# Expert stage of a two-attention, two-expert network: 1/sum on VectorE, variances as columns, single norm pieces, first combination tiles begun in the second sweep

## Chip, core and metric

The kernel runs on one core of one Trainium2 chip. The metric is the device time of one execution in microseconds (us), as the median of several runs. Lower is better.

## What is computed

The reference takes x of 4096 tokens by 256 features, in float32, and adds four branches to it, one after another, each on the layer norm of what came before:

```
x = x + attention_a(layernorm(x))
x = x + experts(layernorm(x))
x = x + attention_b(layernorm(x))
x = x + experts(layernorm(x))
```

Both attentions are causal with 16 heads. The expert branch is the same both times, with the same weights. It has 64 experts with 32 slots each, so 2048 columns in all:

```
logits = (x @ phi_w.T + phi_b).reshape(8, 512, 64, 32)
D = softmax(logits, over the 32 slots)        # dispatch
C = softmax(logits, over the 64 experts)      # combination
X_tilde = clip(einsum('tznp,tzd->npd', D, x), -33000, 65000)
X_tilde = tanh(normalised X_tilde over d: (X - mu) * rsqrt(var + 1e-5))
Y_tilde = einsum('npd,ndH->npH', X_tilde, expert_w) + expert_b
out     = einsum('tznp,npH->tzH', C, Y_tilde)
```

## The kernel before

The 4096 tokens are 32 tiles (NT) of 128 rows (P); x stays on chip. Four stages follow one another: attention a, experts, attention b, experts. Both expert stages run the same class, `_Experts` (lines 607 to 975). The first ends in statistics and queries for attention b; the second writes `out`.

**Order.** TensorE's instructions are kept in the program's order (helpers `mm`, line 66, and `tr`, line 69). All others (VectorE, ScalarE, GpSimd and the DMA issues on SyncE, called SP) are ordered by the framework's scheduler when the kernel is built. It may move an issue ahead of or behind its neighbours. Each engine then runs its own list strictly in order. Pieces of work can be put into a queue, `side`, and `beside` (line 79) takes one piece from it per call.

**Norm and sweeps.** The layer norm of x is cut into pieces of four tiles: statistics (line 91 on), the roots, the scaling on ScalarE, and two transposes of two tiles each. A transpose goes into a bank (line 72), the only one in its PSUM pool, and is copied to `xnT` on ScalarE (line 753). Two groups of four tiles are normed ahead; 36 pieces go into `side`. Then there are two sweeps over the 32 tiles, one for each half h of the 2048 columns. In each step:

- `logits(h, t)` makes 128 x 1024 logits, with the bias added by VectorE (line 775), stores them to DRAM (`ld`), takes the maximum of each expert's slots, subtracts it on GpSimd (line 783), and takes the exp on ScalarE. VectorE also takes the column maxima `cm`.
- `divide(h, t)` sums (line 796), takes the reciprocal and multiplies on GpSimd (line 798).
- Four products accumulate X_tilde in PSUM (`acc`).

Logits run two tiles ahead of the accumulation, divide one. After the first sweep the norm of half 0 of X_tilde and its expert products are pieces beside the second sweep.

**Norm of X_tilde.** `centre` gets the mean over features by a matmul with a matrix of 1/256, subtracts on VectorE and squares on GpSimd. `spread` gets the variance likewise, in all 128 rows at once, and takes the root and, on 128 x 512 elements, the reciprocal (line 702). `squash` multiplies on GpSimd (line 707) and takes tanh. `product(ec)` multiplies 128 slots by the weights of four experts; its result goes through the one bank to `ys` (line 720).

**Combination.** It runs over the 32 tiles:

- `combine_begin(t)` loads the tile's logits `l` back (1 MB, line 805), then the 128 KB of x as it was ahead of the branch, `xl` (line 809), takes the maximum of both halves (`mc`, line 811), subtracts it on GpSimd in two halves (line 815) and takes the exp (line 818).
- `combine_sums(t)` sums over experts on VectorE (`sc`, line 824), takes the reciprocal (line 825), and copies it fourfold on GpSimd (line 827).
- `turn(t)` transposes the reciprocals (`rT`), copies them on ScalarE (line 835), and transposes e in 16 pieces (`ps`). VectorE multiplies both to `lT` (line 842).
- `weigh(t)` multiplies `lT` by `ys` in 16 products; VectorE adds `xl` and writes x (line 860). The second stage then issues the store of `out` (line 862); the first takes statistics.

Begin and sums run two tiles ahead of weigh, turn one. The buffers are two of `l`, three of e, two of `lT`, four of `ps`; `xl` and the small tiles come from a pool with four buffers of each. Tiles 0 and 1 are begun at the second-last step of the second sweep. The first turn and half of the first weigh lie between the steps of half 1's norm.

Of the kernel before, what the change touches and what calls it, by code (L numbers as in the profile page):

```python
# [606 lines left out]
class _Experts:  # L607
# [8 lines left out]
    def __init__(self, net, phiT, phi_b, ew, eb, out=None, attention=None):  # L616
        self.net, self.phiT, self.phi_b = net, phiT, phi_b
        self.ew, self.eb, self.out = ew, eb, out
        self.attention = attention
        self.phi = net.zone[:, 0 : 2 * E].rearrange("p (c e) -> p c e", c=2)  # L620
        self.phb = net.zone[:, 2 * E : 3 * E]

    def load(self):
        nc, EH = self.net.nc, E // 2
        for h in range(2):
            for c in range(2):
                nc.sync.dma_start(
                    self.phi[:, c, ts(h, EH)], self.phiT[ts(c, P), ts(h, EH)]
                )
            nc.sync.dma_start(  # L630
                self.phb[:, ts(h, EH)],
                self.phi_b[ts(h, EH)].rearrange("(o e) -> o e", o=1).partition_broadcast(P),
            )

    def run(self):
# [10 lines left out]
        with ExitStack() as ctx:  # L646
# [4 lines left out]
            sp = pool("ff_s", 4)  # L651
            net.banks = pool("psm", 1, space=PSUM)
# [3 lines left out]
            nc.gpsimd.memset(mean, 1.0 / D)  # L656
            ys = [cp.tile([P, NC2, D], F32, name="ys0"), None]
# [8 lines left out]

            def load_w(ec, w=None):
                if w is None:
                    w = ewp.tile([P, 4, 2, D], F32, name="w")
                nc.sync.dma_start(w, ew[ts(ec, 4)].rearrange("n (c p) h -> p n c h", p=P))  # L670
                ews[ec] = w

            def load_b(h):
                b = rp.tile([P, NC2, D], F32, name="ebt")
                for j in range(4):
                    nc.sync.dma_start(
                        b[ds(32 * j, 32), :, :],
                        eb.rearrange("(o c j) h -> j o c h", o=1, j=4)[j][:, ts(h, NC2), :]
                        .partition_broadcast(32),
                    )  # L680
                ebs[h] = b

            sqs = {}

            def centre(n):
                xs = xt[:, :, ts(n, 512)]
                mu = net.bank()
                for d in range(2):
                    mm(mu, mean, xs[:, d, :], start=d == 0, stop=d == 1)
                sq = ewk.tile([P, 2, 512], F32, name="sq")  # L690
                for d in range(2):
                    nc.vector.tensor_tensor(xs[:, d, :], xs[:, d, :], mu, ALU.subtract)
                    nc.gpsimd.tensor_tensor(sq[:, d, :], xs[:, d, :], xs[:, d, :], ALU.mult)
                sqs[n] = sq

            def spread(n):
                sq = sqs[n]
                var = net.bank()
                for d in range(2):
                    mm(var, mean, sq[:, d, :], start=d == 0, stop=d == 1)  # L700
                nc.scalar.activation(sq[:, 0, :], var, AF.Sqrt, bias=net.eps)
                nc.vector.reciprocal(sq[:, 0, :], sq[:, 0, :])

            def squash(n):
                xs = xt[:, :, ts(n, 512)]
                for d in range(2):
                    nc.gpsimd.tensor_tensor(xs[:, d, :], xs[:, d, :], sqs[n][:, 0, :], ALU.mult)
                nc.scalar.activation(xs, xs, AF.Tanh)

            def product(ec):  # L710
                w = ews.pop(ec)
                y = net.bank()[:, 0:D]
# [20 lines left out]
            def norm_pieces(j):  # L733
                def stats(i2):
                    for t in (4 * j + 2 * i2, 4 * j + 2 * i2 + 1):
                        net.stats(t)
                    if i2:
                        net.roots(4 * j, 4 * j + 4)

                def scale():  # L740
                    for t in range(4 * j, 4 * j + 4):
                        nc.scalar.activation(
                            x[:, t, :], x[:, t, :], AF.Identity,
                            bias=shift[:, t : t + 1], scale=rstd[:, t : t + 1],
                        )

                def turn(i2):
                    t2 = 2 * j + i2
                    pt = net.bank().rearrange("p (c i t) -> p c i t", c=2, i=2)
                    for i in range(2):  # L750
                        for c in range(2):
                            tr(pt[:, c, i, :], x[:, 2 * t2 + i, ts(c, P)])
                    nc.scalar.copy(
                        xnT[:, :, ts(t2, 2 * P)], pt.rearrange("p c i t -> p c (i t)")
                    )

                return [
                    lambda: stats(0), lambda: stats(1), scale, lambda: None,
                    lambda: turn(0), lambda: turn(1),
                ]  # L760
# [4 lines left out]
            def logits(h, t):  # L765
                l = lp.tile([P, NH, SLOT], F32, name="l")
                lf = l.rearrange("p n s -> p (n s)")
                for n in range(2):
                    lg = pl.tile([P, 512], F32, name="lg")
                    for c in range(2):  # L770
                        mm(
                            lg, xnT[:, c, ts(t, P)], phi[:, c, ds(h * EH + n * 512, 512)],
                            start=c == 0, stop=c == 1,
                        )
# [3 lines left out]
                nc.sync.dma_start(ld[t][:, h, :], lf)  # L778
# [22 lines left out]
            ce, css, lTs, xls, pools = {}, {}, {}, {}, {}  # L801

            def combine_begin(t):
                l = pools["l"].tile([P, NEXP, SLOT], F32, name="l")
                nc.sync.dma_start(
                    l.rearrange("p n s -> p (n s)"), ld[t].rearrange("p h e -> p (h e)")
                )
                xl = sp.tile([P, D], F32, name="xl")
                nc.sync.dma_start(xl, xd[:, t, :])
                m = sp.tile([P, SLOT], F32, name="mc")  # L810
                nc.vector.tensor_tensor(m, cm[:, t, 0, :], cm[:, t, 1, :], ALU.max)
                e = pools["e"].tile([P, NEXP, SLOT], F32, name="e")
                for h in range(2):
                    ns = ts(h, NH)
                    nc.gpsimd.tensor_tensor(  # L815
                        e[:, ns, :], l[:, ns, :], _bc(m.unsqueeze(1), [P, NH, SLOT]), ALU.subtract
                    )
                    nc.scalar.activation(e[:, ns, :], e[:, ns, :], AF.Exp)  # L818
                ce[t], xls[t] = e, xl


            def combine_sums(t):
# [4 lines left out]
                nc.gpsimd.tensor_copy(s4, _bc(s.unsqueeze(1), [P, 4, SLOT]))  # L827
# [39 lines left out]
            for j in range(2):  # L867
                for f in norm_pieces(j):
                    f()
            for j in range(2, NT // 4):  # L870
                net.side.extend(norm_pieces(j))
# [4 lines left out]
            for n, (h, t) in enumerate(seq):  # L876
# [7 lines left out]
                if n + 1 < len(seq):  # L884
                    divide(*seq[n + 1])
                if n == len(seq) - 2:

                    nctx.close()
                    pools["e"] = pool("fc_w", 2)
                    pools["l"] = pool("fc_l", 1)  # L890
                    pools["lT"] = pool("fc_t", 1)
# [7 lines left out]
                if n < len(seq) - 2:  # L899
                    for _ in range(2 if h == 0 else 1):  # L900
                        net.beside(3)
# [15 lines left out]
                if n == len(seq) - 2:  # L917
                    assert not net.side and not net.urgent and not net.agenda
                    load_b(1)
                    for k in range(3):  # L920
                        load_w(
                            NC2 + 3 + k,
                            net.zone[:, ts(k, E)].rearrange("p (n c h) -> p n c h", n=4, c=2),
                        )
                    for k in range(2):
                        combine_begin(k)
                        combine_sums(k)
# [4 lines left out]
            load_w(NEC - 2, pool("ff_wx", 1, rctx, side="right").tile([P, 4, 2, D], F32, name="wx"))  # L932
            pools["r"] = pool("fc_r", 1, space=PSUM)
            pools["t"] = pool("fc_p", 4, space=PSUM)
            pools["o"] = pool("fc_o", 2, space=PSUM)
            centre(2)
            centre(3)
            turn(0)
            spread(2)
            spread(3)  # L940
            weigh(0, 0, NC2)
            squash(2)
            squash(3)
            for ec in range(NC2, NEC):
                product(ec)
                if ec == NC2:
                    load_w(NEC - 1)
# [4 lines left out]
            for t in range(NT):  # L952
                if t + 2 < NT:
                    combine_begin(t + 2)
                if t == 0:
                    weigh(0, NC2, NEC)
                if t + 1 < NT:
                    turn(t + 1)
                if t + 2 < NT:
                    combine_sums(t + 2)  # L960
                if t > 0:
                    weigh(t, 0, NEC)
# [104 lines left out]
```

## Time and profile before

| | |
|---|---|
| median of 3 runs | 5329.53 us (5329.0 to 5331.33) |
| the profiled execution's own time | 5322.71 us |
| its span | 5321.0 us |
| granted TensorE clock | 0.983 |
| first expert stage, in the span | about 1780 to 2674 us |
| second expert stage | about 4436 to 5321 us |
| TensorE, VectorE, ScalarE, GpSimd busy | 94, 78, 49, 23% |

The tables and lines of the profile come from one execution. A row of a group has the line of the program, the engine, the operation, what it writes and reads with shapes, the count, then total busy us and the mean in ns, and the idle time of the engine ahead of it with what ended that. PE is TensorE, PEld its weight loads, DVE is VectorE, ACT ScalarE, POOL GpSimd and SPq the DMA issues of SyncE. A row of a window has the stretch in us, its length, the busy us of each engine with its instructions in brackets, the granted clock of TensorE as a share of full speed, the share of time in which the DMA engines worked, and GB/s. A row of the timeline has the start in us, the duration, the engine, and what was done; in square brackets stands how long the engine had been idle and for whom. A row of waits has the sum in us, the count and the longest.

### The profile page before, as it was taken

The page shows a single profiled execution, that of the slowest core. Times are in us where ns is not written, and L with a number is a line of the kernel's source. Part 1 is how long each engine was busy: PE and PEld are TensorE (multiplying, and loading weights), DVE is VectorE, ACT ScalarE, POOL GpSimd, SP SyncE. Part 2 cuts the span into 40 slices and gives each one's busy share as a digit, 9 for nine tenths or more (in the row PEclk, how much of TensorE's full clock was granted, in tenths as well). Part 3 has the DMA queues.
Part 4 walks back from the last instruction along what each step waited for, and adds up shares of the span by engine and source line. Part 5 has one row for each costly group of instructions (what it writes and reads, how often), then busy time and mean ns, then how long its engine had stood idle before and what let it go on. Part 6 is the DMA issues. An engine that isn't in the chain of part 4 may idle for free.

```text
span 5321.0 us, 79263 instructions
## 1 busy us (share of the span) xinstructions
PE 5025.3 (94%) x29824; PEld 2663.5 (50%) x29824; DVE 4142.4 (78%) x7742; ACT 2608.9 (49%) x3036; POOL 1208.7 (23%) x1178
## 2 busy tenths in 40 slices
PE   7999999999999899979989999999999998999799
PEld 4444454545454344447744454444454543444577
DVE  5788998989987478767757888989899864787665
ACT  3566666666677412122235666666666674111221
POOL 3211000000000345454411110000000003455443
PEclk9999999999999999989989999999999999999899
DMA  6433221222211211443353342222222112113432
GB/s 248 140 111 121 74 68 63 69 63 63 62 59 42 85 68 67 138 142 113 119 199 130 105 128 68 66 70 61 63 63 67 56 36 86 67 75 135 143 129 90
DMA packets 265584, 499.16 MB, mean 94 GB/s; under 512 B 44880, under 2 KB 109904, under 8 KB 257008
## 3 DMA queue, kind: packets, MB, share of 16 engines
q1 hardware_dynamic: 259968, 485.57, 27.5%
q10 hardware_dynamic: 4896, 7.87, 0.4%
q8 instruction: 234, 3.83, 0.3%
q14 instruction: 150, 1.23, 0.1%
q0 software_dynamic: 336, 0.66, 0.0%
HBM read 336.73 MB, written 156.76 MB: 93 GB/s over the span
## 4 chain that ended last, share of the span: by engine, by line
PE 65%; DVE 14%; POOL 11%; ACT 4%; issue 4%; DMA 1%; SPq 0%; DVEq 0%; POOLq 0%; ACTq 0%
PE bank L67 20%; PE o L67 20%; PE sc L67 17%; POOL e L815 5%; DVE mx L386 4%; DVE sc L824 4%; PE lg L67 3%; POOL e L783 3%; PE acc L67 3%; DVE junk L380 2%; POOL e L798 2%; ACT e L786 2%; DVE l L775 1%; ACT e L818 1%; ACT pb L462 1%
## 5 line engine op out<-in xcount | busy, mean ns | idle before, releaser
L462 ACT ACTIVATE pb<-sc 128x1024 f32<-128x1024 f32 (+3 forms) x2304 | 2071.0, 951 | 1093.2 <-PE sc L67 1090.3
L386 DVE TENSOR_REDUCE mx<-bank 128x1 f32<-128x512 f32 x3584 | 2223.2, 681 | 169.9 <-PE bank L67 165.7
L67 PE MATMUL bank<-k,q 64*128 64x512 f32 (+3 forms) x4608 | 1350.0, 452 | 72.8 <-DVE mx L386 29.9
L67 PEld LDWEIGHTS bank<-k,q 64*128 64x128 f32 x4608 | 666.5, 185 | 1178.6 <-DVE mx L386 780.3
L67 PE MATMUL o<-pb,va 128*32 128x512 f32 (+3 forms) x9216 | 1158.2, 574 | 0.9 <-POOL pb L466 0.7
L67 PE MATMUL sc<-q,k 64*128 64x512 f32 (+3 forms) x4608 | 988.1, 390 | 9.9 <-ACT pb L462 9.4
L67 PE MATMUL sc<-qm,one 64*128 64x512 f32 (+3 forms) x4608 | 946.9, 376 | 0.0
L466 POOL TENSOR_SCALAR_AFFINE_SELECT pb<-pb 128x256 f32<-128x256 f32 x512 | 205.7, 408 | 2260.5 <-ACT pb L462 2254.8
L380 DVE CUSTOM_DVE_ANT_0 junk<-bank,maskw 128x128 bf16<-128x128 f32 (+3 forms) x1024 | 501.6, 490 | 259.1 <-PE bank L67 151.8
L67 PEld LDWEIGHTS sc<-q,k 64*128 64x128 f32 x4608 | 508.8, 186 | 138.4 <-ACT pb L462 99.8
L67 PEld LDWEIGHTS sc<-qm,one 64*128 64x128 f32 x4608 | 525.6, 186 | 66.6
L786 ACT ACTIVATE e<-e 128x1024 f32<-128x1024 f32 x128 | 135.2, 1056 | 786.3 <-POOL e L783 786.3
L67 PE MATMUL acc<-e,x 128*128 128x512 f32 x1024 | 472.1, 605 | 35.2 <-POOL e L798 33.6
L67 PE MATMUL lg<-zone,xnT 128*128 128x512 f32 x1024 | 469.3, 602 | 0.2
L67 PE MATMUL o<-ys,lT 128*128 128x256 f32 x2048 | 453.0, 379 | 0.0
L67 PEld LDWEIGHTS o<-ys,lT 128*128 128x128 f32 x2048 | 384.5, 190 | 51.8 <-issue 2.0
L818 ACT ACTIVATE e<-e 128x1024 f32<-128x1024 f32 x128 | 135.3, 1057 | 459.3 <-POOL e L815 449.6
L67 PEld LDWEIGHTS acc<-e,x 128*128 128x128 f32 x1024 | 197.9, 194 | 290.5 <-issue 242.4
L798 POOL TENSOR_TENSOR e<-e,s 128x1024 f32<-128x1024 f32 x128 | 244.7, 1913 | 385.7 <-DVE s L797 385.7
L67 PEld LDWEIGHTS o<-pb,va 128*32 128x32 f32 x9216 | 182.9, 108 | 285.8 <-issue 263.2
L67 PEld LDWEIGHTS lg<-zone,xnT 128*128 128x128 f32 x1024 | 194.9, 193 | 242.5 <-issue 229.5
L815 POOL TENSOR_TENSOR e<-l,mc 128x1024 f32<-128x1024 f32 x128 | 299.6, 2363 | 24.1 <-DVE x L860 17.1
(101 smaller groups left out, 3234.9 us busy)
## 6 DMA issues: line engine op xcount, KB each, us to landing
k<-ak SPq DMA_DIRECT2D x144, 512.0 KB
k<-bk SPq DMA_DIRECT2D x144, 512.0 KB
ld<-l SPq DMA_DIRECT2D x128, 512.0 KB
l<-ld SPq DMA_DIRECT2D x64, 1024.0 KB
w<-in_L_ffn_expert_w_dram SPq DMA_DIRECT2D x24, 1024.0 KB
q<-aq SPq DMA_DIRECT2D x32, 512.0 KB
rb<-dd SPq DMA_DIRECT2D x64, 256.0 KB
q<-bq SPq DMA_DIRECT2D x32, 512.0 KB
```

Of the source, the lines that this page charges most:

```text
L67: self.tc.keep_in_program_order(self.nc.tensor.matmul(*a, **k))
L380: nc.vector.tensor_tensor_reduce(out=junk[:, 0:w], in0=scs[h2][:, 0:w], in1=maskw[:, QB - w : QB], scale=1.0, scalar=-3e38, op0=ALU.add, o ...
L386: nc.vector.tensor_reduce(m, scs[h2], AX.X, ALU.max)
L462: nc.scalar.activation(pb[:, :, off:QB], sc[:, :, off:QB], AF.Exp)
L466: nc.gpsimd.affine_select(out=d, in_=d, compare_op=ALU.is_ge, fill=0.0, base=0, pattern=[[0, 2], [1, P]], channel_multiplier=-1,)
L775: nc.vector.tensor_tensor(lf[:, ts(n, 512)], lg, phb[:, ds(h * EH + n * 512, 512)], ALU.add)
L783: nc.gpsimd.tensor_tensor(e, l, _bc(m.unsqueeze(2), [P, NH, SLOT]), ALU.subtract)
L786: nc.scalar.activation(ef, ef, AF.Exp)
L798: nc.gpsimd.tensor_tensor(e, e, _bc(s.unsqueeze(2), [P, NH, SLOT]), ALU.mult)
L815: nc.gpsimd.tensor_tensor(e[:, ns, :], l[:, ns, :], _bc(m.unsqueeze(1), [P, NH, SLOT]), ALU.subtract)
L818: nc.scalar.activation(e[:, ns, :], e[:, ns, :], AF.Exp)
L824: nc.vector.tensor_reduce(s, ce[t].rearrange("p n s -> p s n"), AX.X, ALU.add)
```

## The change

It affects `_Experts` alone. In words:

- The fourfold copy of 1/sum goes from GpSimd to VectorE.
- Layer norm: one piece norms four tiles, one piece transposes two; 20 pieces are queued. The first two transposes use the PSUM buffers of the logits. `beside` is called ahead of the accumulation in each step, and once more behind it in the first sweep.
- Norm of X_tilde: squares on ScalarE; variances as columns of 128 x 1 by tiny matmuls, with root and reciprocal on 128 x 4; they are put on a diagonal on VectorE and spread over the rows by a matmul with ones; VectorE multiplies from PSUM.
- The products of half 1 alternate between two PSUM banks.
- Tile 0 of the combination is begun in step 24 of the second sweep, in memory that half 0 of `phi` has left; tile 1 at the second-last step; tile 2 between the norm of half 1 and its products. In the main loop the beginning and the sums run three tiles ahead instead of two.
- `xl` has a pool of its own with four buffers; `ps` has three buffers instead of four.
- The DMAs of the expert stage, apart from `out` and from the loads of phi, go through a new helper that keeps them in the program's order on SP.

The diff, cut to its core:

```diff
-        self.phi = net.zone[:, 0 : 2 * E].rearrange("p (c e) -> p c e", c=2)
+        self.phi = net.zone[:, 0 : 2 * E].rearrange("p (h c e) -> p h c e", h=2, c=2)
...
+            xlp = pool("ff_xl", 4)
...
+            one = cp.tile([P, P], F32, name="one")
+            nc.gpsimd.memset(one, 1.0)
...
+            def dma(o, i):
+                tc.keep_in_program_order(nc.sync.dma_start(o, i))
...
-                    nc.gpsimd.tensor_tensor(sq[:, d, :], xs[:, d, :], xs[:, d, :], ALU.mult)
+                nc.scalar.activation(sqs[n], xs, AF.Square)
...
-                for d in range(2):
-                    mm(var, mean, sq[:, d, :], start=d == 0, stop=d == 1)
-                nc.scalar.activation(sq[:, 0, :], var, AF.Sqrt, bias=net.eps)
-                nc.vector.reciprocal(sq[:, 0, :], sq[:, 0, :])
+                for k in range(4):
+                    for d in range(2):
+                        mm(
+                            var[:, k : k + 1], sq[:, d, ts(k, P)], mean[:, 0:1],
+                            start=d == 0, stop=d == 1,
+                        )
+                r = sp.tile([P, 4], F32, name="rx")
+                nc.scalar.activation(r, var[:, 0:4], AF.Sqrt, bias=net.eps)
+                nc.vector.reciprocal(r, r)
+                nc.vector.tensor_tensor(
+                    sq[:, 0, :].rearrange("p (k e) -> p k e", k=4),
+                    _bc(net.ident.unsqueeze(1), [P, 4, P]), _bc(r.unsqueeze(2), [P, 4, P]),
+                    ALU.mult,
+                )
...
+                rs = net.bank()
+                mm(rs, one, sqs[n][:, 0, :], start=True, stop=True)
-                    nc.gpsimd.tensor_tensor(xs[:, d, :], xs[:, d, :], sqs[n][:, 0, :], ALU.mult)
+                    nc.vector.tensor_tensor(xs[:, d, :], xs[:, d, :], rs, ALU.mult)
...
-                nc.sync.dma_start(ld[t][:, h, :], lf)
+                dma(ld[t][:, h, :], lf)
...
+            def maxima(t):
+                cms[t] = sp.tile([P, SLOT], F32, name="mc")
+                nc.vector.tensor_tensor(cms[t], cm[:, t, 0, :], cm[:, t, 1, :], ALU.max)
+                xls[t] = xlp.tile([P, D], F32, name="xl")
+                dma(xls[t], xd[:, t, :])
...
+                dma(l.rearrange("p n s -> p (n s)"), ld[t].rearrange("p h e -> p (h e)"))
+                maxima(t)
...
-                nc.gpsimd.tensor_copy(s4, _bc(s.unsqueeze(1), [P, 4, SLOT]))
+                nc.vector.tensor_copy(s4, _bc(s.unsqueeze(1), [P, 4, SLOT]))
...
+            norm(0)
+            norm(1)
+            turn_x(0, first)
+            turn_x(1, first)
+            for j in range(2, NT // 2):
+                if j % 2 == 0 and j > 2:
+                    net.side.append(lambda j=j: norm(j // 2))
+                net.side.append(lambda j=j: turn_x(j))
...
+                if (h, t) == (1, 24):
...
+                    ce[0], l = z(0, E), z(2 * E, EH)
+                    maxima(0)
+                    for h2 in range(2):
+                        dma(l.rearrange("p n s -> p (n s)"), ld[0][:, h2, :])
+                        exponentials(0, ce[0], l, h2)
+                    combine_sums(0)
...
-            pools["t"] = pool("fc_p", 4, space=PSUM)
+            pools["t"] = pool("fc_p", 3, space=PSUM)
...
-                if t + 2 < NT:
-                    combine_begin(t + 2)
+                if t + 3 < NT:
+                    combine_begin(t + 3)
...
-                if t + 2 < NT:
-                    combine_sums(t + 2)
+                if t + 3 < NT:
+                    combine_sums(t + 3)
```

## The prediction

> **What bounds the kernel now.** I read the page first: the share of each engine, then the chain that ended last, to see whether TensorE is short of work or held up.
>
> ```profile
> PE 5025.3 (94%) x29824; PEld 2663.5 (50%) x29824; DVE 4142.4 (78%) x7742; ACT 2608.9 (49%) x3036; POOL 1208.7 (23%) x1178
> ...
> PE 65%; DVE 14%; POOL 11%; ACT 4%; issue 4%; DMA 1%; SPq 0%; DVEq 0%; POOLq 0%; ACTq 0%
> ...
> L815 POOL TENSOR_TENSOR e<-l,mc 128x1024 f32<-128x1024 f32 x128 | 299.6, 2363 | 24.1 <-DVE x L860 17.1
> ```
>
> TensorE is busy 94% of the span, yet the chain runs outside it for 35%, and GpSimd, busy 23% overall, carries 11% of the chain. The last row says where: the combination's exponent on GpSimd hardly ever waits. The change touches only the two expert stages (1780 to 2674 and 4436 to 5321 us), so I asked for windows of the first.
>
> ```profile
> core 0: us, PE busy (x) PEld busy (x) DVE busy (x) ACT busy (x) POOL busy (x), PEclk, DMA share, GB/s
> 1800.00:2050.00 250.00, 231.90 (x569) 106.11 (x570) 184.47 (x203) 44.63 (x51) 121.51 (x66) 0.98 0.23 87
> 2290.00:2350.00 60.00, 35.77 (x219) 20.77 (x218) 29.63 (x35) 10.82 (x12) 22.67 (x17) 0.86 0.39 135
> 2350.00:2460.00 110.00, 94.72 (x499) 81.03 (x499) 87.16 (x109) 35.33 (x45) 60.56 (x37) 0.95 0.39 131
> ```
>
> TensorE idles 18 us of the first sweep, 24 of the transition between the sweeps and the combination, and some 14% of the combination's start. The waits of TensorE name the causes: in the first sweep (first line) the norm's transposes wait for ScalarE's copy out of the one bank; in the combination (other two) for VectorE, and once, 11 us long, for GpSimd's copy.
>
> ```profile
> PE bank L70 <- ACT xnT L753: 14.0, 6, 2.7
> ...
> PE ps L70 <- DVE lT L842: 12.1, 18, 1.0
> PE rT L70 <- POOL s L827: 11.0, 1, 11.0
> ```
>
> Last came the timeline of one combination tile in the second expert stage.
>
> ```profile
> 5198.90 0.36 DVE L860 TENSOR_TENSOR x<-o,xl 128x256 f32<-128x256 f32 x1
> 5199.11 0.29 POOL L827 COPY s<-sc 128x128 f32<-128x128 f32 x1 [5.34 <-DVE sc L825]
> ...
> 5199.29 0.34 SPq L862 DMA_DIRECT2D out_dram<-x  x1
> 5199.36 4.69 POOL L815 TENSOR_TENSOR e<-l,mc 128x1024 f32<-128x1024 f32 x2
> 5199.68 0.43 SPq L809 DMA_DIRECT2D xl<-xd  x1
> ...
> 5204.08 0.32 SPq L805 DMA_DIRECT2D l<-ld  x1
> ...
> 5204.09 1.06 ACT L818 ACTIVATE e<-e 128x1024 f32<-128x1024 f32 x1 [1.27 <-POOL e L815]
> ...
> 5205.17 3.69 DVE L824 TENSOR_REDUCE sc<-e 128x32 f32<-128x2048 f32 x1 [0.89 <-ACT e L818]
> ...
> 5208.90 0.35 DVE L825 RECIPROCAL sc<-sc 128x32 f32<-128x32 f32 x1
> ...
> 5209.17 0.36 DVE L860 TENSOR_TENSOR x<-o,xl 128x256 f32<-128x256 f32 x1
> ```
>
> The period is 5209.17 - 5198.90 = 10.27 us. A ring sets it: exponent on GpSimd 4.69, exp 1.06, sum 3.69, reciprocal 0.35, copy on GpSimd 0.29, hops 0.2; then GpSimd starts the next tile. The load of l was issued 11 us before the next use and is hidden. TensorE alone would need 8.76, from rows of the same tile's work in the first stage: 0.11 + 1.75 + 6.90 between these starts.
>
> ```profile
> 2371.54 0.27 PE L70 MATMUL rT<-ident,s 128*128 128x128 f32 x1
> 2371.65 1.91 PE L70 MATMUL ps<-ident,e 128*128 128x128 f32 x16
> 2373.40 0.81 PE L67 MATMUL o<-ys,lT 128*128 128x256 f32 x3
> ```
>
> (The weigh before it began at 2364.64.)
>
> **The sweeps.** Single norm pieces, two places for them per step: the six waits (14.0) and one of 2.5 for stats go. But GpSimd's two operations (1.92 + 1.91) with the exp and the reduce between them come round every 7.13 us in undisturbed steps (2220 to 2290), and TensorE's 8 + 8 instructions take 6.87. Sweep 1 lasts 243 us (1810 to 2053), 7.59 a step, so at most 32 x (7.59 - 7.13) = 15 us can go; I take 12, and 3 at the start, where the first transposes get other banks: -15. In sweep 2 the norm of X_tilde loses its two wide reciprocals (6.5 us of VectorE) and four products on GpSimd (5.0); tile 0's exponent (4.7) and sum (3.7) come in. Net -2 (between -8, the stalls of TensorE there, and +6, the insertion with nothing hidden). Tile 0's DMAs count too: its second half-load waits for GpSimd, and behind it on SP stand the next steps' stores of l, for some 2.4 + 2.5 us; two buffers of l give a step's 7.1 us of cover, and without it the 5 us would fall on logits, inside the +6. Tiny matmuls (8 of 128x1) have no row; nearest is the 256-column one at 0.09 to 0.38: 1 to 3 us a stage, or 0 in TensorE's stalls; within the -2.
>
> **The transition.** From the last accumulation (2298.4) to the last product (2344.4) are 46 us. The new order still has centre, spread and squash in series, and tile 2's sum (3.7) stands before the products' additions on VectorE, but two banks alternate and wide reciprocal and GpSimd steps go. Tile 2's l waits on SP for tile 1's exponent, with the last expert weights behind it. I take -3.5 (+5 to -14).
>
> Taken at nothing: the squares move to ScalarE (as wide as the exp of 1.06), busy 44.6 us of 250, so covered, else 1 us each; phi's other layout, the constant of ones and the weights in other buffers change no count of instructions; three PSUM buffers for the transposes instead of four let TensorE run 0.6 us less ahead of lT, hidden by its waits below, else 0.6 a tile, 38 us.
>
> Both stages: 2 x (-15 - 2 - 3.5) = -41.
>
> **1/sum on VectorE.** No row: GpSimd's copy takes 0.29, VectorE's 128x32 mc 0.19 and its 128x256 addition 0.36. I take 0.25; 64 x 0.25 = 16 us if VectorE bound the tile, 0 if it waits. It waits below: 0.
>
> **The combination.** Every expert DMA but out is now held in the program's order. In the built order of the changed kernel, SP in the second stage runs l(t), xl(t), out(t-3), l(t+1): behind out(k), which waits for the addition x(k), stand l(k+4) and xl(k+4). Before, the l load stood ahead of these. And VectorE runs sc(k+4) before x(k+1). So a ring replaces the old one: x(k) 0.36, hop 0.03, out's issue 0.39, the load of l, exponent 4.70, hop 0.06, exp 1.06, hop 0.03, sum 3.70, hop 0.03, then x(k+1). The load: 5204.08 to the end of its traffic is 4.1; tile 2's exponents began 5.0 after their load's issue. I take 4.5 (4.1 to 5.1). Sum 14.86 us a tile against 10.27, for the 25 tiles from k = 3 to 28: +115 us (105 to 130). TensorE, with 6 us to spare in it, costs nothing.
>
> A rule weighs on this. No row of before shows whether a waiting out holds the loads behind it. The Trainium skill, page "DMA: Bandwidth & Descriptors", section "Anatomy of one DMA — SWDGE (gpsimd) path", says that transfer engines don't wait on semaphores: a wait is spent on the issuing sequencer, ahead of dispatch. By it everything behind out(k) stands still, +115; were the wait spent in the transfer, the loads would go early and the lookahead of 3 would help: the first rival's sum. I follow the rule.
>
> In the first stage there is no out, but xl(t) takes the buffer of xl(t-4), which x(t-4) frees, and l(t+1) stands behind it: l(k+5) waits for x(k). Built VectorE order differs by tile. Where the sum stands before the addition (sc9 x5, sc10 x6) the ring is as above, 14.9; where the addition comes first (x7 sc11, x15 sc19) two tiles share 26.3; at tiles 16 to 21 the addition, sum, lT, transposes and weigh go one after another: 0.4 + 3.7 + 1.3 + 0.5 + 6.9 = 13. Going through the list by hand gives 13.3 a tile on average over 26 tiles: 26 x (13.3 - 10.27) = +79 (50 to 100).
>
> TensorE's clock is the other rule. In the first stage it fell to 0.50 after an 11 us wait, and 16 transposes took 3.54 us instead of 1.91. The skill, page "TensorE: Matmul & The Clock Gate", section "Part 1: The HAM clock gate (the "warmup" mystery)", puts the threshold at one idle window of some 3.4 us. A 14.86 period leaves 6 us idle, so by the rule each tile pays the 1.6 of this row, 51 x 1.6 = 82 us if on the path. The ring doesn't run through TensorE in the second stage, so I take 0 there, and leave the rest to the high end.
>
> **Sum.** 5322.7 - 41 + 79 + 115 = 5476 for the profiled execution; the median of the runs lies 6.8 above it: 5482 us.
>
> **Rivals.** (1) Faster: the loads get ahead, since three tiles of lookahead and the early start outrun the gate. Then TensorE bounds at some 8.85: 52 x (8.85 - 10.27) = -74, and -41: 5215. The 94% speak for it, the order on SP against. Chance 0.10. (2) No change: sums and additions interleave so that the mean period is 10.27 + 41/51 = 11.07, which pays back exactly the -41. Nothing points at that: 0.03. From that mean on it is slower. (3) The ring binds in one stage only, or loads land sooner: -41 and +80 to +130, 5370 to 5420: 0.15. (4) The ring is longer: a load lands at 5.1 to 6 after issue, or half-clock transposes come onto the path, 0.6 to 1.3 more for 45 tiles: 5510 to 5540: 0.17. My forecast: 0.55.
>
> The measurement can tell about 0.2%, 10.7 us. Faster 0.10, same 0.03, slower 0.87. The range takes in (4) and most of (3): 5390 to 5540.
>
> **What would show it.** In the combination, GpSimd's exponent waits for the DMA of l at each tile, SP issues l directly behind x and out, and additions in the second stage lie 14.9 apart, 443 us from last product to end instead of 328. Wrong, if GpSimd still never waits, or l is issued ahead of out. In the first sweep the waits for ScalarE's copy are gone; if not, the -15 fails.

## The result and the profile after

The changed kernel takes 5526.85 us (median of 4 runs, 5522.55 to 5532.97) against 5329.26 before (4 runs). The ratio is 1.0372, with a 95% interval of 1.0354 to 1.0390: slower by 198 us. Its profiled execution took 5529.21 us, span 5527.4, that is 206.5 more than the one before. The forecast was 5482, range 5390 to 5540.

First the page of the changed kernel: the engines, the chain that ended last, and the group of the combination's exponent (now line 814).

```profile
PE 5097.8 (92%) x29936; PEld 2749.5 (50%) x29936; DVE 4153.3 (75%) x7830; ACT 2614.1 (47%) x3044; POOL 1157.1 (21%) x1084
...
PE 67%; DVE 11%; POOL 7%; DMA 6%; issue 6%; ACT 3%; SPq 0%; POOLq 0%; DVEq 0%; ACTq 0%
...
L814 POOL TENSOR_TENSOR e<-l,mc 128x1024 f32<-128x1024 f32 x124 | 289.6, 2357 | 621.7 <-DMA l<-ld 550.2
```

All three answer to lines shown of before. The share of the DMA in the chain went from 1 to 6%. The exponent, whose engine had idled 24 us ahead of it in all, now idles 622, and 550 of that ends with the landing of `l`. Its own time is unchanged, 2357 ns against 2363.

The windows of the changed kernel answer to those of before: the first sweep, the transition (20 us earlier), the start of the combination, and then the steady combination of the second stage.

```profile
1800.00:2050.00 250.00, 243.02 (x611) 110.88 (x610) 201.31 (x222) 48.39 (x55) 131.18 (x70) 0.99 0.24 87
2270.00:2330.00 60.00, 44.62 (x285) 30.39 (x285) 32.65 (x47) 12.97 (x16) 15.69 (x8) 0.94 0.60 181
2350.00:2460.00 110.00, 84.80 (x396) 72.66 (x396) 65.11 (x94) 24.84 (x31) 37.41 (x16) 0.86 0.23 76
...
5110.00:5496.90 386.90, 276.88 (x1225) 235.94 (x1225) 170.20 (x222) 57.16 (x75) 116.78 (x50) 0.83 0.25 85
```

TensorE is busier in the first two (243 us of 250 instead of 232; 45 of 60 instead of 36, though this window holds 13 us of the sweep and that of before 8), and has clearly more idle time in the combination. GpSimd falls from 60.6 to 37.4 us of 110. The granted clock in the steady second stage is 0.83; it was 1.00 between 5034.6 and 5294 before.

One tile of that stage in the timeline shows the new ring from end to end. By the order of the two lists, the load is that of tile k+4, behind the store of tile k, and the sum is that of k+4, ahead of the addition of k+1.

```profile
5279.30 0.41 DVE L872 TENSOR_TENSOR x<-o,xl 128x256 f32<-128x256 f32 x1
...
5279.74 0.34 SPq L874 DMA_DIRECT2D out_dram<-x  x1
...
5280.19 0.37 SPq L672 DMA_DIRECT2D l<-ld  x1
...
5281.06 8.76 PE L67 MATMUL o<-ys,lT 128*128 128x256 f32 x32
5285.38 4.67 POOL L814 TENSOR_TENSOR e<-l,mc 128x1024 f32<-128x1024 f32 x2 [10.74 <-DMA l<-ld]
...
5290.09 1.06 ACT L817 ACTIVATE e<-e 128x1024 f32<-128x1024 f32 x1 [1.27 <-POOL e L814]
...
5291.18 3.57 DVE L836 TENSOR_REDUCE sc<-e 128x32 f32<-128x2048 f32 x1 [0.90 <-ACT e L817]
5294.67 0.41 DVE L872 TENSOR_TENSOR x<-o,xl 128x256 f32<-128x256 f32 x1
```

Addition, store of out, load of l, exponent, exp, sum, addition: 15.37 us. The load, from issue to the start of the exponent, takes 5.19 of it. TensorE's weigh runs beside that and takes 8.76 us; before it took 7.07. The signs that the prediction named are there: the exponent waits for the load at each tile, the load is issued straight behind the store, the additions lie 15.5 us apart (14.9 foretold), and in the first sweep no wait for ScalarE's copy is left (14.0 us before).

I read the ends of the stretches of each expert stage off the timelines. "Sweep 1" goes from the first accumulation to the first clip, "sweep 2" to the last accumulation, "transition" to the last addition of the products (ys), "combination" to the last addition x. "x to x" is the mean spacing of the additions of tiles 3 to 28. (Before it was 10.27 in the steady part; tile 28 comes early.)

| us, stage a / b | sweep 1 | sweep 2 | transition | combination | x to x |
|---|---|---|---|---|---|
| before | 251.6 / 251.5 | 245.2 / 245.1 | 46.1 / 46.0 | 326.7 / 324.2 | 10.00 / 9.97 |
| after | 232.9 / 233.8 | 244.0 / 246.1 | 42.6 / 40.1 | 444.6 / 461.5 | 14.60 / 15.48 |
| e1_unpinned | 233.6 / 232.8 | 240.1 / 240.7 | 47.0 / 47.7 | 386.2 / 369.1 | 12.54 / 11.90 |
| e4_fetch_xl5 | 233.4 / 232.6 | 246.6 / 245.6 | 40.7 / 40.8 | 403.9 / 414.8 | 13.06 / 13.80 |
| e5_b_s4dve | 251.5 / 251.9 | 245.2 / 245.2 | 46.3 / 47.4 | 303.2 / 290.7 | 8.88 / 8.50 |
| e6_b_pinned | 251.8 / 254.5 | 242.9 / 242.6 | 51.5 / 51.6 | 406.0 / 480.1 | 13.21 / 15.47 |
| e7_b_norm | 232.8 / 232.8 | 233.8 / 233.8 | 46.1 / 48.2 | 326.8 / 324.2 | 10.00 / 9.97 |
| e9_unpinned_ps4 | 233.0 / 232.8 | 240.0 / 240.8 | 48.9 / 48.4 | 292.2 / 283.2 | 8.88 / 8.59 |
| e12_ps4 | 233.2 / 233.4 | 244.3 / 243.1 | 53.1 / 52.3 | 362.1 / 345.4 | 11.66 / 11.28 |
| e14_tile0_late | 233.0 / 232.8 | 237.5 / 237.3 | 52.1 / 51.7 | 294.4 / 283.4 | 8.95 / 8.59 |

So the change gains some 23 us in each stage ahead of the combination, and loses 118 and 137 in the two combinations.

### The profile page after: what moved, and what is told of

Read it like the earlier page. It is cut to its first block, busy times and chain, and to the rows that moved or that the text cites. A ratio compares the mean times of both kernels' runs of the same rounds, so it can differ in the third digit from the quotient of the medians.

```text
span 5527.4 us, 79363 instructions
## 1 busy us (share of the span) xinstructions
PE 5097.8 (92%) x29936; PEld 2749.5 (50%) x29936; DVE 4153.3 (75%) x7830; ACT 2614.1 (47%) x3044; POOL 1157.1 (21%) x1084
## 4 chain that ended last, share of the span: by engine, by line
PE 67%; DVE 11%; POOL 7%; DMA 6%; issue 6%; ACT 3%; SPq 0%; POOLq 0%; DVEq 0%; ACTq 0%
PE bank L67 20%; PE o L67 19%; PE sc L67 16%; PE acc L67 5%; PE lg L67 5%; DMA l<-ld 4%; POOL e L814 4%; DVE mx L386 4%; DVE junk L380 2%; POOL e L792 1%; POOL e L807 1%; DVE sc L836 1%; ACT e L817 1%; ACT pb L462 1%; ACT e L795 1%
## 5 line engine op out<-in xcount | busy, mean ns | idle before, releaser
L67 PE MATMUL o<-ys,lT 128*128 128x256 f32 x2048 | 530.9, 425 | 0.0
L67 PEld LDWEIGHTS o<-ys,lT 128*128 128x128 f32 x2048 | 442.9, 219 | 75.4 <-issue 3.2
L814 POOL TENSOR_TENSOR e<-l,mc 128x1024 f32<-128x1024 f32 x124 | 289.6, 2357 | 621.7 <-DMA l<-ld 550.2
L70 PE MATMUL ps<-ident,e 128*128 128x128 f32 x992 | 153.5, 305 | 223.2 <-DVE lT L854 223.1
```

Source lines behind the costliest of these rows:

```text
L67: self.tc.keep_in_program_order(self.nc.tensor.matmul(*a, **k))
L70: self.tc.keep_in_program_order(self.nc.tensor.transpose(o, i, self.ident))
L814: nc.gpsimd.tensor_tensor(e[:, ns, :], l, _bc(cms[t].unsqueeze(1), [P, NH, SLOT]), ALU.subtract)
```

## The experiments

**Is it the place of the loads in SyncE's list?** Four kernels on this. `e1_unpinned` lets the scheduler place the DMAs again:

```diff
             def dma(o, i):
-                tc.keep_in_program_order(nc.sync.dma_start(o, i))
+                nc.sync.dma_start(o, i)
```

> The changed kernel with one thing undone: the expert stage's DMAs are issued by SyncE without being held in the program's order. My theory (the loads of l stand behind out, and behind xl, which wait for the addition x) expects the combination at 9.1 to 9.7 us a tile in both stages, bounded by TensorE, and GpSimd's exponents without waits for l: some 5 to 6 us a tile less, 5230 to 5290 in all. Rival A (the slowdown is VectorE's: the copy of 1/sum there and the sums ahead of the additions) expects over 5450, since nothing on VectorE is undone. Rival B (three transposing buffers and TensorE at half clock) expects the same, over 5450.

Measured: 5380.46 us, ratio to before 1.0098 (1.0083 to 1.0113). This undoes 146 of the 198 us, so the held order is one cause of the loss, but the forecast of 5230 to 5290 was too low. The tile takes 11.9 us in the second stage, not 9.1 to 9.7, and the trace shows another wait.

```profile
5201.95 2.47 DVE L854 TENSOR_TENSOR lT<-ps,r 128x512 f32<-128x512 f32 x4
...
5202.69 0.66 PE L70 MATMUL ps<-ident,e 128*128 128x128 f32 x4 [1.21 <-DVE lT L854]
...
5203.42 4.67 POOL L814 TENSOR_TENSOR e<-l,mc 128x1024 f32<-128x1024 f32 x2 [7.21 <-PE ps L70]
...
5209.22 3.68 DVE L836 TENSOR_REDUCE sc<-e 128x32 f32<-128x2048 f32 x1 [0.90 <-ACT e L817]
```

GpSimd no longer waits for the load. It waits for the last four transposes of e, whose buffer it needs; those wait for the first lT, which frees one of the three `ps` buffers; and lT stands on VectorE behind the sum of a later tile, which needs the exponent. That is a second ring, of 11.9 us. It lay hidden behind the first. The built order of VectorE moved along with SyncE's list: here the sum of tile k+4 stands ahead of the addition of tile k, in the changed kernel's second stage that of k+3. There it could stand no earlier, since the load of k+4 waits, behind out, for the addition of k.

`e11_l_actq` keeps the program's order on SyncE, but issues the loads of l elsewhere:

```diff
-                dma(l.rearrange("p n s -> p (n s)"), ld[t].rearrange("p h e -> p (h e)"))
+                nc.scalar.dma_start(
+                    l.rearrange("p n s -> p (n s)"), ld[t].rearrange("p h e -> p (h e)")
+                )
```

> The changed kernel with the combination's 1 MB loads of l for tiles 1 to 31 issued by ScalarE instead of SyncE; out, xl and all others stay on SyncE in the program's order. Theory: what hurts is where the load stands in SyncE's list, behind out and xl, so both gates go and only the second ring (three transposing buffers) is left: 11.8 to 12.8 us a tile in both stages, 5360 to 5400, as e1_unpinned. If the load itself were slow or late for another reason (bandwidth, landing), over 5480.

Measured: 5401.79 us, ratio 1.0138 (1.0123 to 1.0153), 2 us above what was expected; 12.48 and 11.84 us from addition to addition. The same transfers, taken out of that list alone, leave only the second ring (VectorE's order is that of e1_unpinned).

`e4_fetch_xl5` keeps all on SyncE, in another program order:

```diff
-            xlp = pool("ff_xl", 4)
+            xlp = pool("ff_xl", 5)
...
                 if t + 3 < NT:
                     combine_begin(t + 3)
+                if t + 4 < NT:
+                    fetch(t + 4)
```

(`fetch` issues the load of l, which `combine_begin` then uses.)

> The changed kernel with the DMAs still held in the program's order, but that order made better: the load of l for tile t+4 stands ahead of the weigh of tile t and so ahead of out(t), and xl has five buffers instead of four. My theory expects both gates gone: 9.2 to 10 us a tile in the second stage, in the first likewise, but for some five tiles (16 to 20) where the built order of VectorE still puts the sum behind the addition, 5240 to 5300. If it isn't where out and xl stand but that the order is held at all (each issue waiting for the one ahead of it), over 5400. Rivals A (VectorE) and B (buffers, clock): over 5450.

Measured: 5440.55 us, ratio 1.0211 (1.0194 to 1.0228): 86 less than the changed kernel, but not 5240 to 5300. Part of the miss is the second ring, 12.3 us in most tiles of the first stage. The other part I had overlooked: out(t-1) still stands ahead of l(t+4), so the gate only moved by one tile. In the second stage the spacings alternate between 11.2 and 15.8 us: the sum that a late load holds stands ahead of every other addition.

`e2_xl5` has only the five buffers of xl:

> The changed kernel with five buffers of xl instead of four, nothing else. Theory: in the first stage l(t+1) stands behind xl(t), which waits for the addition of tile t-4; with five buffers it waits for one tile earlier, and only the second ring of 12.3 us is left there (but for some five tiles whose sum stands behind the addition): 40 to 60 us less. The second stage, where out holds the loads, stays at 15.5 us a tile. 5465 to 5490. If xl's buffers play no part, no change from the changed kernel.

Measured: 5495.67 us, ratio 1.0311 (1.0295 to 1.0326), 6 us above the upper end. The second stage stayed at 15.40 us. The first fell from 14.60 to 13.25: 12.3 in most tiles, but 17.6 to 19.9 in four of those where attention b's first `bk` stores and queries come in. In the changed kernel's trace, at 2581.05, such a store is issued just ahead of a load of l; it had waited for VectorE's piece of attention b at 2580.34, which stands behind the sum there. That is a third gate on the list, and five buffers don't move it. One round of it in the changed kernel:

```profile
2571.05 4.67 POOL L814 TENSOR_TENSOR e<-l,mc 128x1024 f32<-128x1024 f32 x2 [26.04 <-DMA l<-ld]
...
2576.85 3.58 DVE L836 TENSOR_REDUCE sc<-e 128x32 f32<-128x2048 f32 x1 [0.90 <-ACT e L817]
...
2580.34 0.69 DVE L173 TENSOR_TENSOR zone<-bank,zone 128x512 fp32r<-128x512 f32 x1
...
2581.05 0.54 SPq L175 DMA_DIRECT2D bk<-zone  x1
...
2581.69 0.56 SPq L672 DMA_DIRECT2D l<-ld  x1
...
2582.79 8.02 PE L67 MATMUL o<-ys,lT 128*128 128x256 f32 x32
2590.24 2.35 POOL L814 TENSOR_TENSOR e<-l,mc 128x1024 f32<-128x1024 f32 x1 [14.52 <-DMA l<-ld]
```

Exponent, exp, sum, piece of attention b, its store, load, exponent: 19.2 us. The load takes 8.55 of them (7.0 to 8.6 in the four loads that stand behind such stores, against some 5.3 in the other tiles; no run here shows why). The weigh runs beside it.

**Does the held order alone cost that much?** `e6_b_pinned` is the kernel before, with the helper `dma` for ld, l, xl, w and ebt, and nothing else.

> The kernel before with only one part of the change: the expert stage's DMAs (not out) are held in the program's order. Theory: this part alone makes the whole loss. In the second stage l(k+3) stands behind out(k) and the sum of k+3 ahead of the addition of k+1 on VectorE, the same ring of 15 to 15.6 us a tile; in the first stage xl's four buffers gate l(k+5), 12.5 to 14.6 a tile. With nothing gained in the sweeps, 5500 to 5560. Rivals A and B expect no change from before, 5320 to 5340.

Measured: 5568.62 us, ratio 1.0454 (1.0438 to 1.0470), 9 us over the upper end. 15.47 us a tile in the second stage, 13.21 in the first, without any other part of the change. Each transition is also some 5.5 us longer, which the expectation had left out.

**Three transposing buffers.** `e9_unpinned_ps4` and `e12_ps4` both have four buffers and one bank for the products, the first without the held order, the second with it:

```diff
-            pools["t"] = pool("fc_p", 3, space=PSUM)
+            pools["t"] = pool("fc_p", 4, space=PSUM)
...
-            two = pool("fc_x", 1, space=PSUM)
...
-                product(ec, (net.bank, lambda: two.tile([P, 512], F32, name="bank2"))[ec % 2])
+                product(ec)
```

> The kernel of e1_unpinned with one more part undone: four PSUM buffers for the transposes of e instead of three (the products' second bank goes for it). Theory after the first runs: behind the loads lies a second ring. The exponent of tile t+3 needs the buffer of e that the last transposes of tile t free; with three buffers the fourth group of transposes waits for the first lT of its tile, which stands on VectorE behind the sum of a later tile, which needs that exponent. With four buffers all 16 transposes go ahead of lT and the ring is open: 8.8 to 9.1 us a tile as in e5_b_s4dve, 5190 to 5230. Rival (the lookahead of 3 or the copy on VectorE makes the 12 us a tile): no change from e1_unpinned, 5365 to 5395.

Measured: 5200.25 us, ratio 0.9757 (0.9741 to 0.9774). With both rings open a tile takes 8.88 and 8.59 us, TensorE's own time: in the second stage it is busy for all of the 170 us from 4980 to 5150. The sums, the lT and the additions follow each other on VectorE in steady tiles as in e1_unpinned, so here the buffers act by themselves (the bank for the products acts in the transition only, which is 1 to 2 us longer). The first rival's sum (5215) comes near this time.

> The changed kernel with four PSUM buffers for the transposes and the DMAs held in the program's order as they were. Theory: the ring through out and the load of l doesn't run through the transposes, so the second stage stays at 15.2 to 15.6 us a tile; the first stage may gain where tiles go in series: 5490 to 5535. Rival (three buffers are the whole loss): under 5300.

Measured: 5352.52 us, ratio 1.0051 (1.0035 to 1.0066). My expectation fell, and the rival's too. SyncE's list is the same as in the changed kernel. But with four buffers the scheduler built another order on VectorE: in the second stage the addition now stands ahead of the sum in every other tile. The trace shows what that does.

```profile
5153.82 0.42 DVE L872 TENSOR_TENSOR x<-o,xl 128x256 f32<-128x256 f32 x1 [4.08 <-PE o L67]
...
5154.73 0.37 SPq L672 DMA_DIRECT2D l<-ld  x1
...
5158.32 3.75 DVE L836 TENSOR_REDUCE sc<-e 128x32 f32<-128x2048 f32 x1 [0.90 <-ACT e L817]
5159.77 4.67 POOL L814 TENSOR_TENSOR e<-l,mc 128x1024 f32<-128x1024 f32 x2 [2.58 <-DMA l<-ld]
...
5165.74 3.68 DVE L836 TENSOR_REDUCE sc<-e 128x32 f32<-128x2048 f32 x1
5169.34 0.41 DVE L872 TENSOR_TENSOR x<-o,xl 128x256 f32<-128x256 f32 x1
```

From 5153.82 to 5169.34 the ring is there as before, 15.5 us, with the load behind out. The next addition comes 4 to 7 us later, since no sum stands ahead of it. Two tiles share one ring, 11.3 us each. So the price of the gate is set by both lists: the load behind the addition on SyncE, and how many sums stand ahead of additions on VectorE. The buffers changed the second list; that they did is read from the built order and from the spacings, and no kernel here turns that order alone. With the single bank each transition is 10 to 12 us longer than in the changed kernel, and the two combinations save 199 us.

So neither part is the whole cause. Undone alone in the changed kernel, the held order gives back 146 us and the three buffers (with their second bank) 174; both together give back 327. In the kernel before, with four buffers, the held order alone costs 242 (e6_b_pinned).

**The other parts, one by one.** `e5_b_s4dve` is the kernel before with `nc.vector.tensor_copy` for `nc.gpsimd.tensor_copy`.

> The kernel before with only the fourfold copy of 1/sum moved to VectorE. Theory: GpSimd's wait for the sum leaves the ring that sets 10.27 us a tile, so TensorE and its waits for lT bound it at 9.2 to 9.8: 52 tiles save 25 to 55 us, 5275 to 5305. Rival A (the copy on VectorE is what costs) expects 5340 or more.

Measured: 5277.51 us, ratio 0.9906 (0.9891 to 0.9921). This part alone is a gain: it takes the sum and the copy out of GpSimd's ring, and the tile falls from 10.00 and 9.97 us to 8.88 and 8.50.

> The changed kernel with the fourfold copy of 1/sum back on GpSimd. Theory: the ring of 15.5 us doesn't run through this copy, so 5515 to 5540, as the changed kernel. Rival A (the copy on VectorE costs 0.5 us a tile on the path): 5495 to 5510.

Measured (the changed kernel with that one word turned back): 5513.66 us, ratio 1.0347 (1.0332 to 1.0363). That is 13 us below the changed kernel, between the two expectations. The intervals of the two ratios overlap (1.0354 to 1.0390 and 1.0332 to 1.0363), so the copy on VectorE costs little of the 198 us, if anything.

`e7_b_norm` is the kernel before with `norm`, `turn_x`, their queue and the two places of `beside`.

> The kernel before with only the layer norm's pieces of the change: one piece norms four tiles, one transposes two, the first two transposes in the logits' PSUM buffers, one place for a piece ahead of the accumulation and one behind it in the first sweep. My prediction's step says 15 us less in each expert stage, 30 in all: 5290 to 5305. The rival, that the loop through GpSimd and VectorE bounds the sweep anyway, expects 5315 to 5330.

Measured: 5266.18 us, ratio 0.9884 (0.9869 to 0.9899): twice the expected gain. Sweep 1 lost 18.7 us in each stage, and sweep 2, which I hadn't counted here, 11.3.

> The kernel before with two parts of the change together: the copy of 1/sum on VectorE (e5_b_s4dve alone: 49 us less) and the layer norm's pieces (e7_b_norm alone: 61 us less). They act in different stretches, so my theory expects the sum, 5205 to 5230. If the two hide each other, over 5235.

Measured: 5203.87 us, ratio 0.9767 (0.9752 to 0.9781), 1 us below the range. That is 126 us less than before, against 111 for the two parts alone. The gains add up; whether they do more than that, the intervals leave open.

`e14_tile0_late` moves tile 0 of the combination in e9_unpinned_ps4 from step 24 to the second-last step:

```diff
-                if (h, t) == (1, 24):
...
                 if n == len(seq) - 2:
...
+                    ce[0] = net.zone[:, 0:E].rearrange("p (n s) -> p n s", s=SLOT)
+                    l = pools["l"].tile([P, NEXP, SLOT], F32, name="l")
+                    dma(l.rearrange("p n s -> p (n s)"), ld[0].rearrange("p h e -> p (h e)"))
+                    maxima(0)
+                    for h2 in range(2):
+                        exponentials(0, ce[0], l[:, ts(h2, NH), :], h2)
+                    combine_sums(0)
```

> The kernel of e9_unpinned_ps4, with tile 0 of the combination begun at the second-last step of the second sweep, beside tile 1, instead of in step 24. In e7_b_norm, which has no insertion, the second sweep took 234 us from its first to its last accumulation, in the changed kernel 244 and 246. Theory: the insertion costs that sweep some 10 us in each stage and gives less back in the transition: 5 to 20 us less than e9_unpinned_ps4, 5180 to 5196. Rival (tile 0's work is only moved, and its turn then waits in the transition): 5200 to 5215.

Measured: 5204.07 us, ratio 0.9764 (0.9747 to 0.9780). The rival was right: sweep 2 is 3 us shorter, the transition 3 longer. The early start of tile 0 is worth nothing either way. e9_unpinned_ps4, e13_b_s4_norm and e14_tile0_late can't be told apart; all three beat both kernels by over 2% of before. The smallest edit among them is e13_b_s4_norm.

## Why the prediction held

**Ring of the second stage: right, one term too short.** Foretold 14.86 us a tile, measured 15.48 (15.37 in the tile shown). The load of l was taken at 4.5 from a spread of 4.1 to 5.1; it took 5.19, in the tile shown and in the median of 26. The 0.7 covers the 0.62 a tile, 15.5 us over the 25 tiles. The stage's combination lost 137, 115 were foretold; some 7 of the 22 between them come from before, which took 9.97 on average over these tiles and not 10.27, since tile 28 comes early. The rule that decided the forecast, that a wait is spent on the issuing sequencer (the Trainium skill, page "DMA: Bandwidth & Descriptors", section "Anatomy of one DMA — SWDGE (gpsimd) path"), stands there in a section on GpSimd's DMAs; for SyncE's it is borne out by the runs: the load of l is issued 0.45 us behind out's issue, never ahead of it, and e11_l_actq, which takes only the loads off the list, drops the spacing from 15.48 to 11.84.

**First stage: right in most tiles, wrong in the middle ones.** Foretold 13.3 a tile and +79, measured 14.60 and +118. Where the sum stands ahead of the addition, single tiles took 15.2 to 15.8 instead of 14.9, and six of seven pairs 27.0 to 29.0 instead of 26.3; the load's median there was 5.29 instead of 4.5. The larger part of the miss is tiles 16 to 21, six at 13 in the sum. Two took 14.5 and 11.3, the other four 17.7 to 19.8: 24 us more than foretold. That step had the wrong path. I had put the addition, the sum, lT, the transposes and the weigh in series; in the first three of these four the ring is the third gate shown at e2_xl5, through the exponent, the sum, a piece of attention b, its store and the load behind that; the fourth waits for the last of these loads and for two sums. I had not named these stores, and the weigh is not in the ring: it runs beside the load.

**Ahead of the combination: the sum right, the terms not.** Foretold -41, measured -46. Sweep 1: 15 was called the most that its steps could lose; it lost 18.7 and 17.7. My window began at 1810 and left out the first 8 us of a sweep of 251.6, so a step took 7.86 on average and not 7.59, and against 7.13 some 23 could go. Sweep 2: -2 foretold, -1.2 and +1.0 measured, but as the sum of two larger parts, so that it came near is luck. e7_b_norm shows that the norm's pieces, with the place for a piece ahead of the accumulation, take 11 us off it; the insertion of tile 0 and the new norm of X_tilde give that back. The table splits this: with the DMAs free (e1_unpinned) sweep 2 takes 240, so the held order costs some 4 to 5 there (not so in the kernel before, where it alone makes sweep 2 some 2 us shorter, by e6_b_pinned); with the insertion late as well (e14_tile0_late) 237.4, so its place costs 3; the 3.6 from there to e7_b_norm's 233.8 were not separated further. Transition: -3.5 foretold, -3.5 and -5.9 measured.

**1/sum on VectorE at nothing: nearly.** 0.25 us was taken, and 0.21 is what it took in the second stage. e8_s4pool puts the whole part at 13 us at most, in the changed kernel.

**Three buffers at nothing: wrong, though it didn't show in the sum.** The argument was that TensorE's waits hide them. In the order as built that holds: the ring behind them, 11.9 us, is shorter than the one through the load. But they cost 180 us with the loads free (e1_unpinned against e9_unpinned_ps4), and 174 in the changed kernel itself (e12_ps4), where VectorE's built order changes with them. The prediction read its ring from the built order of the changed kernel, which had their effect in it; so the sum came out in spite of this term.

**Clock: right.** In the second stage the granted clock fell to 0.83, and weighs took 8.76 instead of 7.07, 1.7 more where the prediction's rule put 1.6 on a tile (no run here tests the threshold itself). The ring doesn't run through TensorE, and the tile took what the ring's own terms add up to.

**The rivals.** What came is the fourth, the longer ring, which was given 0.17: 5527 lies in its 5510 to 5540, and the load took 5.2 and more, as it says; the third gate it doesn't name. The figure of 5482 was 45 too low, and the range held since it took that rival in. The second and third are out, as the ring stands in both stages. For the first, the loads did not get ahead; had they, that rival's 5215 would still have been 165 too low, by e1_unpinned's 5380. It left out the second ring.

**A reading.** The load of l in before was said to lead its next use by 11 us. With two buffers it is used by the exponent after the next, two periods on: issued at 5204.08, used some 15.8 later. Nothing in the sum rests on it.

## What to carry to other kernels

A DMA queue that is held in the program's order hands every load the waits of all that stands ahead of it. So, ahead of such a step, write the queue's list down, mark which entry waits for what, and ask of each load how long before its use it can still be issued. Then follow the list of the consuming engine as well, since the ring's price hangs on which sum stands ahead of which addition. When a ring is opened, the next one has its own period, here 15.5, then 11.9, then 8.8 us a tile: look for it ahead of summing the gain.

## What the runs showed of the hardware

VectorE's copy of 128x128, the fourfold 1/sum, takes 0.21 us or some six times that. Here are the group in the second stage of the changed kernel, and in that of e9_unpinned_ps4 (the three durations are least, median and largest, in ns).

```profile
L839 DVE COPY s<-sc x32: 210/214/2245, 4983.9 to 5498.1; 128x128 f32<-128x128 f32 x32
```

```profile
L839 DVE COPY s<-sc x29: 213/1234/2408, 4928.1 to 5164.5; 128x128 f32<-128x128 f32 x29
```

In the first GpSimd mostly stands idle, waiting for l, when the copy runs. In the second GpSimd's exponent (4.69 us) runs at that moment. In the tile at 5049.33 the copy begins at 5050.53, takes 1.24 us, and so ends at 5051.77, as the first of the two exponents does (its exp starts at 5051.72). That is so throughout the trace: 53 of the 64 copies begin while an operation of GpSimd runs, and each of them ends 0.08 to 0.09 us after that operation; the ten that meet none take 0.21 to 0.23. So the copy's end is tied to the end of GpSimd's operation, however early it began. The reciprocal keeps its 0.35 beside the exponent, and the sums that lie beside GpSimd's operations take a median of 3.74, those that meet none 3.72. The Trainium skill, page "SBUF — State Buffer", section "🔬 SBUF: two separate sides", says that some operations of VectorE and those of GpSimd share a pair of ports, which one of them holds for a whole instruction while the other stands still; the times agree with that, and show the copy as one of these operations and the sum and the reciprocal as not. It was a rule that spoke against moving the copy, and the prediction didn't weigh it. The price stays hidden: with the slow copies e9_unpinned_ps4 still runs at TensorE's pace.
